# Two attention layers in one pass: normalizations placed by a sum of ScalarE's work, group means in phases of their own, tasks not cut at a unit's end, products of zeros at the start, an earlier last reciprocal

## The chip, the core and the metric

The kernel runs on one core of a Trainium2 chip, as one launch. The metric is the device time in microseconds (us) of that launch. In the profile PE is TensorE's matrix multiplication, PEld its weight loads, ACT is ScalarE, DVE is VectorE, POOL is GpSimd, and SP is the engine whose queue issues most of the DMA transfers. The clock given with the profile is the share of full speed that TensorE was granted.

## What is computed

The input is x of shape (4, 256, 64, 64) in float32. Two layers are applied, each behind a group normalization over 32 groups of 8 channels, each with 8 heads of 32 channels, each added to its input:

```
x = x + layer0(group_norm(x))
    q = Wq.h                      (256 -> 256, at 4096 positions)
    k, v = 2x2 convolutions of h, stride 2   (1024 positions)
    k = k + rel_h + rel_w
    out = softmax(q.k / sqrt(32)) . v        (4096 x 1024 per head)
x = x + layer1(group_norm(x))
    q, k, v = 1x1 projections of h + bias
    attention inside each of 4 areas of 1024 positions
    out = out + depthwise 7x7 convolution of v + bias
    out = Wproj.out + bias
```

## The kernel before, in words

**Units and phases.** Layer 0 of a batch is called ("A", b), layer 1 ("B", b). The order is A0 to A3, then B0 to B3. Each of these eight blocks has 16 units, one for 512 queries of four heads, so there are 128 units. A unit has 8 steps, one for each 128 keys. The main loop runs over phases, 683 of them, and a phase does one step and a half: a full step (512 queries) and a half step (256 queries). So a unit ends in about every fifth phase.

In one phase TensorE makes the scores (tile `s`, L400, three pairs of PSUM banks). ScalarE turns them into exponentials (`p`, L442 twice and L453 once). TensorE then multiplies the previous phase's exponentials with v (tile `av`, L467), and VectorE adds exponentials up (`acc`, L477). Where the previous phase's parts belong to two units, the phase has a cut: the first unit's av ends, ScalarE copies it out (`av_sb`, L1099), and the second unit's av begins. Later the sums are reduced by a product with ones (`den`, L486), copied (`den_sb`), turned into reciprocals by way of DRAM on POOL's queue, and multiplied in.

**Side work.** The projections q, k, v, the output projection (`ops`), the values for the convolution (`vals_ps`) and the convolution itself (`conv_ps`) are tasks. A task has two or four parts. A part is four products of 512 columns, or the same amount in another shape. Between the scores and av of a phase the loop does a number of parts of the task in front; `side_parts(n)` does up to n parts of one task. How many is decided from `pressure()` (what the due times demand), `supply()` (what will be there to do) and a credit. A phase with den does no other part. Side tasks write one PSUM bank, av another; where a cut comes and no task is begun, the two banks change roles (`banks.reverse`), so that the new unit's av need not wait for the copy.

**What feeds the tasks.** Each task reads a normalized chunk. A normalization is one ScalarE instruction (`taps`, `hq`, `hv`, `h`, L364), listed in `norms_left` with a first phase; `norm_next()` does the first one that is due, once at the end of each phase. A task is ready a phase after its last normalization. The group statistics come from `bn_stats` (L543, L656) and are joined in `plan_norm`: aggregation on VectorE, a product with `gmat` for the group means (`gm`, L334), a copy, three VectorE steps, a second product (`gv`, L342), then the power, the product and the sign on POOL. The two products are put in the list `quick`, and the loop takes one at a phase's end where no task is begun.

**Queues.** The order on every engine is the order in which the loop writes instructions. SP's queue is in order too, and carries the chunk loads (`xs`, `xa`, `hq`, `xc`, `hv`, `cv`, `xm`, six buffers of one pool), the layer 1 loads, the stores, and the convolution's rows and bands (`load_share`, issued inside `convolve`). A convolution is ready when both its shares were loaded at least 4 phases ago (`chained`).

**The end.** `project_last` calls `divide` for the last unit, which takes the reciprocal of the last den (L496, one VectorE instruction over 512 columns), multiplies, and the last projection follows.

These few lines stand at the loop's end, and the change replaces them:

```
        if quick and not begun():
            quick.popleft()()
        ...
        norm_next()
        for _ in range(max(parts, 2) - 2 if f < 12 else 0):
            norm_next()
```

Of the kernel before, what the change touches and what calls it, by code (L numbers as in the profile page):

```python
# [15 lines left out]
P = 128  # L16
# [44 lines left out]
def direct_path(  # L61
# [89 lines left out]
    gmat = gmat.rearrange("p g e -> p (g e)")  # L151
    neghalf = const.tile([P, CT], FP, name="neghalf")
    G.memset(neghalf, -0.5)
    ones = const.tile([P, HD], FP, name="ones")
    G.memset(ones, 1.0)
    eps = const.tile([P, 1], FP, name="eps")
# [27 lines left out]
    def at(g, j, f):  # L184
        g, j = g + int(j // NKT), int(j % NKT)
        plan.setdefault((g, j), []).append(f)
# [68 lines left out]
    def advance():  # L255
        side[0][0] -= 1
        side[0][2] = True
        next(side[0][1], None)
        if side[0][0] == 0:
            side.popleft()  # L260

    def need(made, key):
        while key not in made:
# [6 lines left out]
        return bool(side) and side[0][2]  # L270

    norms_left, norm_done = [], {}

    def later(token, f, start=0, first=False):

# [37 lines left out]
    def stats_of(key):  # L313
        if key not in stats:
            stats[key] = pool.tile([P, CT, NCH, 6], FP, tag="st", name=f"st_{key[0]}{key[1]}", bufs=2)
        return stats[key]

    def plan_norm(key, g, j):

        name = f"{key[0]}{key[1]}"  # L320
        made = {}

        def aggregate():
            for tag, cols in (("mv", 2), ("gmean", 1), ("dev", 1), ("gvar", 1)):
                shape = [P, CT, cols] if cols > 1 else [P, CT]
                made[tag] = pool.tile(shape, FP, tag=tag, name=f"{tag}_{name}", bufs=2)
            mv = made["mv"]
            for t in range(CT):
                V.bn_aggr(out=mv[:, t, :], in_=stats[key][:, t].rearrange("p c s -> p (c s)"))

        def means():
            mv, mean, dev = made["mv"], made["gmean"], made["dev"]
            ps = ps_side(f"gm_{name}")[:, :CT]
            T.matmul(ps, lhsT=gmat, rhs=mv[:, :, 0], start=True, stop=True)  # L334
            S.copy(mean, ps)
            V.tensor_sub(dev, mv[:, :, 0], mean)
            V.tensor_mul(dev, dev, dev)
            V.tensor_add(dev, dev, mv[:, :, 1])

        def variances():  # L340
            ps = ps_side(f"gv_{name}")[:, :CT]
            T.matmul(ps, lhsT=gmat, rhs=made["dev"], start=True, stop=True)  # L342
            S.activation(made["gvar"], ps, AF.Identity, bias=eps)
            norm = pool.tile([P, 2, CT], FP, tag="norm", name=f"norm_{name}", bufs=8)
            shift, rstd = norm[:, 0, :], norm[:, 1, :]
            G.tensor_tensor(rstd, made["gvar"], neghalf, ALU.pow)
            G.tensor_tensor(shift, made["gmean"], rstd, ALU.mult)
            G.tensor_scalar(shift, shift, -1.0, None, ALU.mult)
            norms[key] = shift, rstd

        at(g, j, aggregate)
        at(g, j + 1, lambda: soon(means))
        at(g, j + 3, lambda: soon(variances))

    def normalize(key, dst, src, t, by_vector=False):
        while key not in norms:
# [134 lines left out]
    def divide(g, unit):  # L491

        if g == len(units) - 1:

            rb = pool.tile([P, CH], FP, tag="p", name="rb", bufs=PB)
            V.reciprocal(rb, dens[g])  # L496
            V.tensor_mul(unit[4]()[:, unit[0], :], avs.pop(g), rb)  # L497
            spare.extend((dens.pop(g), rb))
            return
        den_sb = pool.tile([P, CH], FP, tag="cout", name="den_sb", bufs=2)  # L500
        few = pool.tile([P, 2, CH // HD], FP, tag="few", name="few", bufs=2)
        rows = dram.tile([4, CH], FP, tag="rows", name=f"rows_{g}", bufs=4)
        S.copy(den_sb, dens.pop(g))
        G.dma_start(rows, den_sb[0:P:HD, :])
        G.dma_start(few[:, 0, :], rows.rearrange("h (q n) -> (h q) n", n=CH // HD))  # L505
        made = {}

        def reciprocals():
            rb = made["rb"] = pool.tile([P, CH], FP, tag="rb", name="rb", bufs=1)
            recs = dram.tile([4, CH], FP, tag="recs", name=f"recs_{g}", bufs=4)  # L510
            V.reciprocal(few[:, 1, :], few[:, 0, :])
            V.tensor_reduce(sums[:, :, g], few, AX.X, ALU.add)  # L512
            G.dma_start(recs.rearrange("h (q n) -> (h q) n", n=CH // HD), few[:, 1, :])  # L513
            for h in range(4):
                G.dma_start(rb[HD * h : HD * h + HD, :], recs[h : h + 1, :].to_broadcast([HD, CH]))  # L515

        def multiply():
            V.tensor_mul(unit[4]()[:, unit[0], :], avs.pop(g), made["rb"])  # L518

        at(*((g + 2, 1) if g < len(units) - 2 else (g + 1, 6)), reciprocals)  # L520
        at(g + 2, 6 if g < len(units) - 2 else 0, multiply)
# [7 lines left out]
    def plan_a(b, u, prep):  # L529

        key = ("A", b)

        early = prep - (5 if b == 1 else 7 if b else 0)
        areas = {}

        seen = {}
# [66 lines left out]

        for c in range(NCH):
            at(early + c // 2, 4 * (c % 2), lambda c=c: look(c))
            at(early + c // 2, 4 * (c % 2) + (6 if b else 3), lambda c=c: add_stats(c))
        plan_norm(key, early + 4, 3 if b > 1 else 4 if b else 1)
        for a in range(NAREA):
            g = prep + (1 + 3.6 * a if b == 1 else 0.05 + 3.7 * a if b else 6 + 2.2 * a)
            at(0, int(NKT * (g - 2.4)), lambda a=a: load(a))  # L610
# [432 lines left out]
    def plan_conv(b, n, start):  # L1043
        when = int(start * NKT)
        room = 3 if b else 2
        for _ in range(room if n == 0 else 0):
            at(0, when - 8, lambda: len(loaded) < room and load_share(True))
        def chained():
            return all(k in loaded and loaded[k][2] + 4 <= phase[0] for k in ((b, 2 * n), (b, 2 * n + 1)))

        task_at(when, 2, convolve, b, n, due=start + 2.5, ready=chained, lag=3)

    units = []
    for i, (layer, b) in enumerate(BLOCKS):
# [38 lines left out]
        if weights_left[g] <= 2 * (NKT - 1):  # L1093
            opened.add(g)

    def evict(g):
        if weights_left[g] == 0 and g in av_of:
            avs[g] = pool.tile([P, CH], FP, tag="av", name="av_sb", bufs=2)
            S.copy(avs[g], av_of.pop(g))  # L1099

# [31 lines left out]
    while f < PHASES or before or plan or side or quick or norms_left or to_add or to_divide:  # L1132
# [13 lines left out]
            accumulate(s, u)  # L1146
        if cut:
            evict(before[0][0] // NKT)
        exps[2]()
        _, rate = pressure()  # L1150
        parts = 0
        if due and not begun():
            g = to_divide.popleft()
            divisors(g, *([last - 1] if g == final else []))
            if g < final:
                divide(g, units[g])
        else:
            wanted = credit + max(min(supply(), 2.0), min(rate, 2.0))
            if rate > 2:
                parts = side_parts(4)  # L1160
            elif rate > 1.5 or due or f >= PHASES or wanted >= (0.8 if cut else 1.5):
                parts = side_parts(2)
            elif wanted >= 0.5 and not cut or begun():
                parts = side_parts(1)
            credit = max(-0.5, min(wanted - parts, 0.5))
# [4 lines left out]
        add_ready()  # L1170
        if f >= PHASES:
            side_parts(2)
        if quick and not begun():
            quick.popleft()()
        while step < -(-3 * (f + 1) // 2):
            do(*divmod(step, NKT))
            step += 1
        norm_next()
        for _ in range(max(parts, 2) - 2 if f < 12 else 0):
            norm_next()  # L1180
        if before:
            evict(before[-1][0] // NKT)
        before = mine
# [599 lines left out]
```

## Time and profile before

| what | us |
|---|---|
| median of 4 runs | 3131.12 (3128.14 to 3135.19) |
| the profiled execution | 3126.19 |
| its span, from the first to the last instruction | 3124.5 |
| mean granted TensorE clock | 0.995 |
| TensorE waits: gm for mv, once, at the start | 17.1 |
| conv_ps for rows, 5 times | 10.6 |
| s for p (L442), 15 times | 10.5 |
| av for av_sb, 18 times | 8.7 |
| mean of one exponential of 1024 columns (L442) | 1.025 |
| mean of one add of 1024 columns (L477) | 1.219 |
| mean of one normalization: taps, hq, hv, h | 0.652, 0.846, 0.840, 1.263 |
| mean of a copy: av_sb, den_sb | 0.592, 0.607 |

A line of the timeline has the start, the length, the engine, the source line, the operation, what is written and read, the shape, and how many records in a row; in brackets the engine's idle time before it and what ended that. Each product stands as two records. Starts of consecutive lines show the pace better than their lengths, since one instruction's end overlaps the next one's start.

### The profile page before, as it was taken

How to read it: one execution, taken by the hardware profiler on the slowest of the kernel's cores; microseconds unless marked ns; L12 is line 12 of the kernel's file. 1: busy time of each engine (PE TensorE's matmuls, PEld its weight loads, DVE VectorE, ACT ScalarE, POOL GpSimd, SP SyncE). 2: the span in 40 equal slices, each digit the busy share in tenths (PEclk: the TensorE clock that was granted, in tenths of full speed). 3: DMA queues.
4: the chain of work that ended last, by engine and by line, in shares of the span. 5: the costliest groups of instructions: out<-in, count | busy, mean ns of one | idle time of the engine just before them, and what ended most of it. 6: DMA issues, size and time to landing. Idle time of an engine off the chain costs nothing. (4 is left out here: it accounts for less than half of the span.)

```text
span 3124.5 us, 109786 instructions
## 1 busy us (share of the span) xinstructions
PE 3043.3 (97%) x47138; PEld 1257.4 (40%) x47138; DVE 2518.0 (81%) x2719; ACT 2456.1 (79%) x2988; POOL 482.7 (15%) x923
## 2 busy tenths in 40 slices
PE   7999999999999999999999999998999999999997
PEld 3444344443344444344344444443434343333332
DVE  3788988778887787778688887776888888888888
ACT  3888888887888888878788787785777877778885
POOL 0111121111211111111112111111111111111111
PEclk9999999999999999999999999999999999999999
DMA  5244433555344466777767567667755465542232
GB/s 187 58 100 102 109 93 83 113 137 145 87 121 133 129 175 168 178 199 190 198 167 183 160 161 193 163 165 177 172 134 129 117 158 131 141 109 73 56 69 61
DMA packets 648322, 423.70 MB, mean 136 GB/s; under 512 B 411772, under 2 KB 556636, under 8 KB 647832
## 3 DMA queue, kind: packets, MB, share of 16 engines
q1 hardware_dynamic: 619384, 380.11, 47.9%
q0 software_dynamic: 28448, 36.48, 4.9%
q8 instruction: 378, 6.19, 0.9%
q14 instruction: 112, 0.92, 0.1%
HBM read 318.32 MB, written 98.09 MB: 133 GB/s over the span
## 5 line engine op out<-in xcount | busy, mean ns | idle before, releaser
L477 DVE TENSOR_TENSOR acc<-acc,p 128x1024 f32<-128x1024 f32 x1790 | 2114.1, 1219 | 457.6 <-PE av L467 220.4
L442 ACT ACTIVATE p<-s 128x1024 f32<-128x1024 f32 x1194 | 1160.4, 1025 | 445.6 <-PE s L400 429.6
L453 ACT ACTIVATE p<-s 128x1024 f32<-128x1024 f32 x598 | 618.8, 1035 | 1.3 <-DVE acc L477 0.8
L400 PE MATMUL s<-q,k_B 32*64 32x512 f32 (+1 forms) x10912 | 547.8, 498 | 8.1 <-ACT p L442 7.0
L400 PE MATMUL s<-q,k_A 32*64 32x256 f32 (+1 forms) x10928 | 546.6, 497 | 5.3 <-ACT p L442 3.5
L467 PE MATMUL av<-p,v_A 128*32 128x256 f32 (+1 forms) x4784 | 453.1, 488 | 0.0
L467 PE MATMUL av<-p,v_B 128*32 128x512 f32 (+1 forms) x4776 | 449.6, 487 | 0.0
L400 PEld LDWEIGHTS s<-q,k_B 32*64 32x64 f32 x10912 | 261.3, 130 | 348.4 <-issue 146.1
L400 PEld LDWEIGHTS s<-q,k_A 32*64 32x64 f32 x10928 | 261.5, 130 | 341.1 <-issue 140.5
L515 POOL DMA_DIRECT2D rb<-recs x508 | 252.1, 502 | 497.6 <-DMA recs<-few 411.9
L513 POOL DMA_DIRECT2D recs<-few x127 | 70.0, 551 | 1361.7 <-DVE sums L512 1202.2
L467 PEld LDWEIGHTS av<-p,v_B 128*32 128x32 f32 x4776 | 149.7, 110 | 261.4 <-issue 235.7
L467 PEld LDWEIGHTS av<-p,v_A 128*32 128x32 f32 x4784 | 152.0, 110 | 234.2 <-issue 194.7
L442 ACT ACTIVATE acc<-s 128x1024 f32<-128x1024 f32 x172 | 167.1, 1023 | 86.8 <-PE s L400 86.8
L505 POOL DMA_DIRECT2D few<-rows x127 | 71.4, 562 | 472.6 <-DMA rows<-den_sb 464.8
L486 PE MATMUL den<-acc,ones 128*32 128x512 f32 x1024 | 140.1, 606 | 2.8 <-DVE acc L477 2.7
L165 PE MATMUL ops<-cv,wp_sb 128*32 128x512 f32 x1024 | 126.5, 605 | 7.1 <-DVE cv L793 4.4
L165 PE MATMUL q1ps<-h,wqkv_sb 128*32 128x512 f32 x1024 | 126.6, 605 | 4.6 <-DVE xm L808 4.6
L165 PE MATMUL k0ps<-taps,wkv 128*32 128x256 f32 x2048 | 125.0, 385 | 2.5 <-ACT taps L364 2.5
L165 PE MATMUL k1ps<-h,wqkv_sb 128*32 128x512 f32 x1024 | 123.9, 597 | 1.8 <-ACT k_B L710 1.6
L165 PE MATMUL q0ps<-hq,wq_sb 128*32 128x512 f32 x1024 | 125.3, 598 | 0.0
L165 PE MATMUL vals_ps<-hv,wqkv_sb 128*32 128x512 f32 x1024 | 123.4, 597 | 0.0
(99 smaller groups left out, 2122.6 us busy)
## 6 DMA issues: line engine op xcount, KB each, us to landing
rows<-vals SPq DMA_DIRECT2D x384, 195.9 KB
rb<-recs POOLq DMA_DIRECT2D x508, 64.0 KB, 3.6
share<-vals SPq DMA_DIRECT2D x128, 195.9 KB
vala<-vout SPq DMA_DIRECT2D x128, 144.0 KB
vals<-vout SPq DMA_DIRECT2D x128, 144.0 KB
vc<-vala SPq DMA_DIRECT2D x64, 288.0 KB
band<-mats SPq DMA_DIRECT2D x96, 176.0 KB
hq<-in_x SPq DMA_DIRECT2D x32, 512.0 KB
```

The costliest lines, as they stand in the source:

```text
L165: T.matmul(out[cols, :], lhsT=lhsT[:, cols], rhs=rhs, start=start, stop=stop)
L400: T.matmul(out[n : n + WIDE], lhsT=unit[2]()[rows, unit[0], j * P + n : j * P + n + WIDE], rhs=unit[1]()[rows, cols], start=True, stop=True,)
L442: S.activation(p, (a, b)[n], AF.Exp, scale=SCALE)
L453: S.activation(p, c.rearrange("p b (l n) -> p b l n", l=2), AF.Exp, scale=SCALE)
L467: T.matmul(out, lhsT=v[:, j, unit[0] * P + HD * h : unit[0] * P + HD * h + HD], rhs=rhs, start=(j == 0 and not u), stop=(j == NKT - 1), sk ...
L477: V.tensor_add(to, to, p)
L486: T.matmul(dens[g][HD * h : HD * h + HD, :], lhsT=ones, rhs=p(h), start=(n == 0), stop=(n == len(sets) - 1),)
L505: G.dma_start(few[:, 0, :], rows.rearrange("h (q n) -> (h q) n", n=CH // HD))
L513: G.dma_start(recs.rearrange("h (q n) -> (h q) n", n=CH // HD), few[:, 1, :])
L515: G.dma_start(rb[HD * h : HD * h + HD, :], recs[h : h + 1, :].to_broadcast([HD, CH]))
```

## The change

It makes these edits, all in the planning code; the products, exponentials and transfers are the same ones, apart from the products of zeros.

- **Account.** `copies` counts ScalarE's extra instructions of a phase (task ends, den, av copies, normalizations), and `behind` carries over what did not fit. `busy(products)` is the sum in us: 0.65 for each, 0.2 for the phase, less 0.857 for each side part. At a phase's end normalizations are done while `busy` with one more (0.75) stays within 0.3 plus 0.1 for each one listed; in the first 20 phases, in the last ones, or when 4 parts or fewer are ready to be done, one is done in any case.
- **Group means.** A `quick` entry takes the place of side work in a phase without den, without a begun task and without a cut, instead of being added to a phase.
- **No half task ahead of a unit's end.** If the begun task has an odd number of parts left, one part is done. In the phase before a cut, two parts are done or none.
- **Products of zeros.** For A0 alone, 44 products of a 128 x 128 tile of zeros are placed ahead of the first group product, and 14 more around the two group products. A0's shift is made by one VectorE instruction in place of two on POOL.
- **Last reciprocal.** It is written where the last den is made.
- **Plan.** For batches 2 and 3 the statistics' loads start one unit earlier, and for these the `bn_stats` stand two steps later behind their loads; the group products are placed accordingly. A convolution waits 6 phases behind its loads instead of 4, and is expected 5 phases later instead of 3.

```
+    idle = const.tile([P, P], FP, name="idle")
+    V.memset(idle, 0.0)
...
         if side[0][0] == 0:
             side.popleft()
+            copies[0] += 1
...
+    def busy(products, more=0.0):
+        return max(0.0, behind[0] + 0.2 + copies[0] * 0.65 + more - 0.857 * products)
...
+    def keep_busy(n):
+        ps = ps_pair("idle")[:, 0, :P]
+        for _ in range(n):
+            T.matmul(ps, lhsT=idle, rhs=idle, start=True, stop=True)
...
+            if key == ("A", 0):
+                V.scalar_tensor_tensor(shift, made["gmean"], -1.0, rstd, ALU.mult, ALU.mult)
+            else:
                 G.tensor_tensor(shift, made["gmean"], rstd, ALU.mult)
                 G.tensor_scalar(shift, shift, -1.0, None, ALU.mult)
...
+        if key == ("A", 0):
+            at(g - 1, 0, lambda: keep_busy(44))
         at(g, j, aggregate)
-        at(g, j + 1, lambda: soon(means))
-        at(g, j + 3, lambda: soon(variances))
+        at(g, j + 1, lambda: soon(lambda: quietly(means, 4)))
+        at(g, j + 3, lambda: soon(lambda: quietly(variances, 10)))
...
-            rb = pool.tile([P, CH], FP, tag="p", name="rb", bufs=PB)
-            V.reciprocal(rb, dens[g])
-            V.tensor_mul(unit[4]()[:, unit[0], :], avs.pop(g), rb)
-            spare.extend((dens.pop(g), rb))
+            V.tensor_mul(unit[4]()[:, unit[0], :], avs.pop(g), spare[1])
...
-        early = prep - (5 if b == 1 else 7 if b else 0)
+        early = prep - (5 if b == 1 else 8 if b else 0)
...
-            at(early + c // 2, 4 * (c % 2) + (6 if b else 3), lambda c=c: add_stats(c))
-        plan_norm(key, early + 4, 3 if b > 1 else 4 if b else 1)
+            at(early + c // 2, 4 * (c % 2) + (6 if b == 1 else 8 if b else 3), lambda c=c: add_stats(c))
+        plan_norm(key, early + (5 if b > 1 else 4), 1 if b != 1 else 4)
...
-            return all(k in loaded and loaded[k][2] + 4 <= phase[0] for k in ((b, 2 * n), (b, 2 * n + 1)))
-        task_at(when, 2, convolve, b, n, due=start + 2.5, ready=chained, lag=3)
+            return all(k in loaded and loaded[k][2] + 6 <= phase[0] for k in ((b, 2 * n), (b, 2 * n + 1)))
+        task_at(when, 2, convolve, b, n, due=start + 2.5, ready=chained, lag=5)
...
             if g < final:
                 divide(g, units[g])
+            else:
+                rb = pool.tile([P, CH], FP, tag="p", name="rb", bufs=PB)
+                V.reciprocal(rb, dens[g])
+                spare.extend((dens.pop(g), rb))
+        elif quick and not begun() and not cut and f < PHASES:
+            quick.popleft()()
         else:
             wanted = credit + max(min(supply(), 2.0), min(rate, 2.0))
...
+            elif begun() and side[0][0] % 2:
+                parts = side_parts(1)
+            elif boundary(mine):
+                parts = side_parts(2) if wanted >= 0.9 else 0
             elif wanted >= 0.5 and not cut or begun():
                 parts = side_parts(1)
...
-        if quick and not begun():
+        if quick and f >= PHASES:
             quick.popleft()()
...
-        norm_next()
-        for _ in range(max(parts, 2) - 2 if f < 12 else 0):
-            norm_next()
+        if before:
+            evict(before[-1][0] // NKT, True)
+        work = max(parts, done_den)
+        force = f >= PHASES or f < 20 or pressure()[0] <= 4
+        while norms_left and (force or busy(work, 0.75) <= 0.3 + 0.1 * len(norms_left)) and norm_next():
+            copies[0] += 1
+            force = f >= PHASES
+        behind[0], copies[0] = min(busy(work), 0.4), 0
```

## Prediction

> **What bounds the kernel now.** I read the page's busy shares, then TensorE's waits, then TensorE's timeline phase by phase.
>
> ```profile
> PE 3043.3 (97%) x47138; PEld 1257.4 (40%) x47138; DVE 2518.0 (81%) x2719; ACT 2456.1 (79%) x2988; POOL 482.7 (15%) x923
> ```
>
> TensorE is the bound, so only what shortens its own sequence counts. The loop has 683 phases. I took each from its first score product (s) to the next phase's. A phase with one side part (den included) takes 3.794 us (the median, 261 phases in program order), with two parts 4.653 (399), with none 3.173 (17); within a kind most agree to 0.01 us. So a second part adds 0.859, a first on top of the bare 3.794 - 0.859 = 2.935 likewise, and a phase without side work wastes 3.173 - 2.935 = 0.238: there the exponentials set the pace. Phases run from 72.4 to 3093.5. Summed at these prices (conv and k0/v0 parts, 0.01 to 0.06 dearer, at their own) they come to 2945.8; the trace has 3021.2. The other 75.3 us lie in some 70 places. The first kind is a half task ahead of a unit's end:
>
> ```profile
> 2606.16 1.58 PE L400 MATMUL s<-q,k_B 32*64 32x256 f32 x32
> 2607.67 1.06 PE L165 MATMUL k1ps<-h,wqkv_sb 128*32 128x512 f32 x8
> 2608.55 1.47 PE L467 MATMUL av<-p,v_B 128*32 128x512 f32 x16
> 2609.95 1.58 PE L400 MATMUL s<-q,k_B 32*64 32x256 f32 x32
> 2611.46 0.64 PE L467 MATMUL av<-p,v_B 128*32 128x256 f32 x8
> 2611.92 1.04 PE L165 MATMUL k1ps<-h,wqkv_sb 128*32 128x512 f32 x8
> 2613.60 1.07 PE L467 MATMUL av<-acc,v_B 128*32 128x512 f32 x8 [0.65 <-ACT av_sb L1099]
> 2614.60 1.58 PE L400 MATMUL s<-q,k_B 32*64 32x256 f32 x32
> ```
>
> The first phase lasts 2609.95 - 2606.16 = 3.79. In the second the task's other half holds the side bank, so the new unit's av must wait until the old one is copied out: 4.65 for one part, 0.85 too much. There are 16 such cuts, 0.42 to 0.85 each, together 10.5 us. Second, the phase behind one without side work:
>
> ```profile
> 1683.75 1.58 PE L400 MATMUL s<-q,k_B 32*64 32x256 f32 x32
> 1685.26 1.06 PE L467 MATMUL av<-p,v_B 128*32 128x512 f32 x8
> 1686.14 0.61 PE L467 MATMUL av<-acc,v_B 128*32 128x256 f32 x8
> 1686.92 1.12 PE L400 MATMUL s<-q,k_B 32*64 32x256 f32 x16 [0.17 <-ACT p L442]
> 1688.33 1.09 PE L400 MATMUL s<-q,k_B 32*64 32x512 f32 x16 [0.29 <-ACT acc L453]
> ...
> 1691.63 1.58 PE L400 MATMUL s<-q,k_B 32*64 32x256 f32 x32
> ```
>
> The empty phase takes 3.17, the next, with den alone, 4.71 instead of 3.79: ScalarE is behind, and its scores wait twice. This follows every one of the empty phases: eight with den next cost 0.85 on average, seven with other work next 0.43, one followed by another empty one 0.19; together 10.0. Third, the convolution waits for its rows:
>
> ```profile
> 1514.29 1.06 PE L1023 MATMUL conv_ps<-share 88*32 88x128 f32 x32
> 1520.27 0.66 PE L1023 MATMUL conv_ps<-rows,band 88*32 88x128 f32 x8 [4.92 <-DMA rows<-vals]
> 1523.03 1.52 PE L1023 MATMUL conv_ps<-rows,band 88*32 88x128 f32 x24 [2.10 <-DMA rows<-vals]
> 1526.18 1.81 PE L400 MATMUL s<-q,k_A 32*64 32x256 f32 x32
> ```
>
> This phase (from 1512.33) takes 13.85 for 4.72, with the one at 1346.8 and its successor 16.1 in all; part of it is the clock, 0.67 of full speed in 1520 to 1530. The rest: 12 group products, 7.0; a stall chain at 2127 to 2155 (VectorE sits 10.3 for vc<-vala, then ScalarE for VectorE), 13.8; den waiting for VectorE's adds at 698.9 and 1571.3, 6.6; a normalization waiting for hv near 1478, 2.7; small ones 8.6.
>
> **The change, part by part.** Places are counted in the two programs' instruction orders; work is equal but for products of zeros.
>
> Half tasks (the odd-remainder and boundary branches): cuts with one part fall from 16 to 1. 10.5 - 0.4: -10.1.
>
> The price stands beside it: phases without side work rise from 17 to 41, since parts are held back at boundaries and means and variances get phases of their own. 24 x 0.238 = 5.7. Behind them: 13 have den next (13 x 0.85 = 11.1), 17 other work (17 x 0.43 = 7.3), 10 an empty one (10 x 0.19 = 1.9), one ends the loop: 20.3 less 10.0 = +10.3. Together +16.0. The lower bound is +5.7, if the account keeps ScalarE from being behind; the upper 24 x (0.238 + 0.85) = +26. I take the rows' own prices, because ScalarE's new order still has av_sb, den_sb and a normalization side by side at four of the 13, as at three of the rows of 0.91 now.
>
> Group products: of the 12, 11 get empty phases and one stays beside two parts. Now they cost 0.31 to 0.33 beside two parts, 0.55 to 1.20 beside den or one part, where they wait for a bank that is still to be copied (496.84: 0.70 behind den_sb). In an empty phase no bank is pending. 12 x 0.15 = 2 left, between 0 and 12 x 0.31 = 3.7: -5 (-7 to -3).
>
> Convolution (lag 5, chained +6): loads in program order lie at least 4 phases before use now (20 of 128 at 4), then at least 5, all but one 6 and more. Two phases are at least 2 x 3.79 = 7.6; the longest overrun is 4.92 + 2.10 = 7.0. That covers it, with the same SP order around: -14 (-16 if nothing remains, -5 if the transfers are later still). Its tasks stretch (phases 305 to 400 for the second batch, 296 to 376 now), and none comes within 20 phases of its first reader except the last batch, where five phases remain before cv<-conv is issued.
>
> Statistics for b of 2 and 3: xs loads one unit earlier, bn_stats two steps later. VectorE's wait of 2.39 for xs at 694.7 precedes the 5.1 at 698.9: -4 (0 to -6.6). The cost is a chunk slot held two steps longer; behind it on SP's queue stand hq, hv, cv and xm, which need slots of that pool.
>
> Normalizations by the account: one per phase now, later only when ScalarE's sum allows it or few tasks are pending. Behind a late one wait the tasks that read it. Two show it: q0 of batch 3 is forced inside a score group at phase 277 (new; the other forced place shrinks from three tasks to two), and at five places two tasks share a phase. The nearest row is 0.81 (k1ps waiting for k_B, near 2181): +2 (0 to +4). The gain for the hv wait: -1 (0 to -2.7).
>
> The chain at 2127: the change touches neither vc<-vala nor its place; convolutions stand at phases 449, 455, 462 as against 448, 454, 461. It depends on how late SP is: -4 (0 to -13.8).
>
> Head. The two first k0 blocks take 8.71 for 2 x 3.63: 1.45 of cold clock; gm and gv 0.56 + 0.59 for 0.38 each: 0.39; two POOL steps (20.31 to 20.83) against one on VectorE, idle until the result, of 0.16: 0.36. Best -2.2. A zero product costs between 0.23 (a 256-column k0 product, 3.63/32, times four for four strips, halved) and 0.37 (two weight loads of 0.186), double while cold. From about 1 us, 44 of them end between 13 and 19, and gm is due at 17.08: up to +2 if late. I take -1. [...]
>
> Tail: the reciprocal goes ahead of the 0.75 step that waits for TensorE:
>
> ```profile
> 3102.77 1.16 DVE L793 SCALAR_TENSOR_TENSOR cv<-cv,bpe_sb,att_B 128x512 f32<-128x512 f32 x1
> 3104.89 0.75 DVE L808 SCALAR_TENSOR_TENSOR xm<-ops,bproj_sb,xm 128x512 f32<-128x512 f32 x1 [0.97 <-PE ops L165]
> 3105.56 3.35 DVE L496 RECIPROCAL rb<-den 128x512 f32<-128x512 f32 x1
> ```
>
> Only the idle 0.97 goes, since both steps still precede att: -1 (to -2.7 if the clock then stays up).
>
> Sum: -10.1 + 16.0 - 5 - 14 - 4 + 2 - 1 - 4 - 1 - 1 = -22.1. Against the profiled execution's 3126.19 (span 3124.5 and 1.7 around it): 3104.1. The median of the runs, 3131.12, is 4.9 above that execution: 3109.
>
> **Rivals.**
> 1. The transfers all come right: the 2127 chain and the adds vanish too (-13.8 - 6.6 - 2.7 for the -9 above): 14 less, 3095. For it: fewer loads in flight at once. Against: SP's order near 2127 is the same.
> 2. A wash: empty phases at +26, conv at -5, group products at -3. 22.1 - 10 - 9 - 2 leaves -1, 3130. For it: 41 empty phases are a large count. Against: those prices are the ends.
> 3. Slower: normalizations held back keep chunk slots, SP's in-order queue stands, and transposes come late as at 2127. The place would be batches 2 and 3 of the first layer, phases 250 to 400, where SP also waits now (391.8 us for out<-xm alone). One such chain is 13.8; two eat the gain, and three give 3131.1 - 22.1 + 41.4 = 3150. It decides from the second. Against: SP's waits mostly hide, and the conv spacing relieves the queue there.
> 4. Zero products do nothing or harm: 3 us at most, inside the range.
>
> **How the numbers follow.** About 0.2% (6 us) is what this kernel's measurement can tell from no change. Forecast 0.52, its own range 3095 to 3122; rival 1, 0.20; rival 2, 0.14; rival 3, 0.14. The range reaches to rival 1's further side, and over rival 2's time: 3088 to 3133. Faster: 0.52 + 0.20 and a third of rival 2: 0.77; same 0.09; slower 0.14.
>
> **What would show it.** TensorE's list of waits: av for av_sb near 2 us (8.7 now); conv for rows under 2 (10.6); scores for p up, to some 20 (10.5), each behind an empty phase. k0's first 128 records near 7.3. The half-clock windows at 1352 and 1520 gone. Wrong if scores wait less for p than now (empty phases are cheap: 3095), or if conv, or VectorE for vc, waits 10 us or more somewhere new (rival 3).

## The result, and the profile after

The changed kernel takes 3131.93 us (median of 49 runs, 3126.14 to 3140.72) against 3131.01 for the kernel before (74 runs beside them): ratio 1.0005, 95% interval 1.0000 to 1.0011. Forecast were 22 us less; there is no gain that can be measured. The profiled execution has a span of 3132.6 us, 8.1 above the one of before, whose own time lay 4.9 below its median.

The busy shares of the page of after:

```profile
PE 3068.4 (98%) x47254; PEld 1270.8 (41%) x47254; DVE 2517.8 (80%) x2721; ACT 2458.0 (78%) x2988; POOL 483.9 (15%) x921
```

ScalarE and VectorE work as long as before, within 2 us; nothing was added that costs by itself. PE is busier by 25 us, 18.5 of them the products of zeros at the start. So the answer is in the waits. TensorE's list of waits, after (what waited, for what; us in all, times, the longest):

```profile
PE s L423 <- ACT p L465: 23.8, 22, 6.2
PE den L509 <- DVE acc L500: 6.0, 4, 3.3
PE k1ps L167 <- ACT k_B L730: 3.0, 3, 1.4
...
PE gm_B L347 <- DVE mv_B L342: 2.0, 2, 1.0
...
PE av L490 <- ACT av_sb L1122: 0.6, 1, 0.6
```

Two signs came as foretold: av waits 0.6 us for its copy instead of 8.7, and the convolution's wait for rows (10.6) has left the list. The scores wait 23.8 us for p; about 20 were foretold, but 16.3 of them are three single waits, of 5.2, 6.2 and 4.8 us, and none of them comes behind an empty phase. ScalarE's own list of waits for data, after, names what they are:

```profile
ACT hv L387 <- DMA hv<-xmid: 11.5, 4, 6.5
ACT hq L387 <- DMA hq<-in_x: 7.1, 2, 6.0
ACT hv L387 <- POOL norm_B L364: 6.0, 1, 6.0
```

Before, the only such wait above 1.6 us was for hv (7.6 in all, the longest 3.9). The longest of after, in ScalarE's and then TensorE's timeline:

```profile
1380.84 0.61 ACT L523 COPY den_sb<-den 128x512 f32<-128x512 f32 x1
1387.95 0.81 ACT L387 ACTIVATE hv<-hv,norm_B 128x512 f32<-128x512 f32 x1 [6.50 <-DMA hv<-xmid]
1388.67 1.92 ACT L465 ACTIVATE p<-s 128x1024 f32<-128x1024 f32 x2
```

```profile
1380.58 1.58 PE L423 MATMUL s<-q,k_A 32*64 32x256 f32 x32
1382.09 1.06 PE L167 MATMUL vals_ps<-hv,wqkv_sb 128*32 128x512 f32 x8
1382.97 1.47 PE L490 MATMUL av<-p,v_A 128*32 128x256 f32 x16
1390.64 2.04 PE L423 MATMUL s<-q,k_A 32*64 32x256 f32 x20 [6.19 <-ACT p L465]
```

ScalarE's order is fixed, so a normalization whose chunk has not landed holds up the exponentials behind it (6.50 us here), and the scores wait for their banks (6.19). The prediction's wait for conv_ps was TensorE's own; this one is the same stall one engine further on.

The whole loop, taken phase by phase with the prediction's prices (3.173, 3.794, 4.653 for none, one and two parts); what a phase takes above its price goes to the row of what it waited for. In us, one profiled execution each:

```
                                        before   after
head (to the first phase)                 72.4    72.0
phases at their prices                  2942.9  2948.4
cuts with a half task                      9.7     0.8
convolution waits for rows                15.3     0
ScalarE waits for late data                3.9    22.5
VectorE waits for a transfer              21.4    16.7
the phase behind an empty one              8.2    16.4
phases with group products                 7.8     8.9
all else above the price                  12.0    17.2
tail                                      30.9    29.7
span                                    3124.5  3132.6
```

The row of ScalarE counts the phases in which it waits for a transfer or for `norm_B`, the scale and shift that the group products lead to; the longer phase right behind such a stall is not in it. So 5.3 of the 22.5 us are the wait for `norm_B` at 507, where the kernel before has 1.5 of its 3.9. The phases are sorted anew here, so a row can differ from the prediction's by up to 2 us.

These are single executions, and rows may shift by a few us: the first group mean alone begins between 15.96 and 18.15 us in the executions profiled here, as the first loads land. The kernel before had medians from 3116 to 3133 us on the chips used, so the experiments are compared by their ratio to the kernel before on the same chip; the rows of the table serve to see where the time lies. The changed kernel was not timed beside the experiments, so what one edit is said to be worth in it is a difference of two ratios, 1.0005 and the experiment's, and rests on the ratio being the same on every chip. Two experiments on one chip can be set against each other without that.

### The profile page after: what moved, and what is told of

It reads as the page before. It is cut to its first block, busy times and chain, and to the rows that moved or that the text cites. A ratio compares the mean times of both kernels' runs of the same rounds, so it can differ in the third digit from the quotient of the medians.

```text
span 3132.6 us, 110020 instructions
## 1 busy us (share of the span) xinstructions
PE 3068.4 (98%) x47254; PEld 1270.8 (41%) x47254; DVE 2517.8 (80%) x2721; ACT 2458.0 (78%) x2988; POOL 483.9 (15%) x921
## 3 DMA queue, kind: packets, MB, share of 16 engines
q8 instruction: 378, 6.19, 0.8%
## 5 line engine op out<-in xcount | busy, mean ns | idle before, releaser
L423 PE MATMUL s<-q,k_A 32*64 32x256 f32 (+1 forms) x10928 | 556.0, 501 | 23.8 <-ACT p L465 21.5
```

The lines of the kernel that those rows point to most:

```text
L423: T.matmul(out[n : n + WIDE], lhsT=unit[2]()[rows, unit[0], j * P + n : j * P + n + WIDE], rhs=unit[1]()[rows, cols], start=True, stop=True,)
```

## The experiments

Four undo one part of the change (the diffs are against the changed kernel). First the account:

```
-        if before:
-            evict(before[-1][0] // NKT, True)
...
-        behind[0], copies[0] = min(busy(work), 0.4), 0
+        norm_next()
+        for _ in range(max(parts, 2) - 2 if f < 12 else 0):
+            norm_next()
```

> The changed kernel, with the old rule for normalizations (one at each phase's end) in place of the account. Late-data theory (the account writes normalizations into ScalarE's in-order stream before their chunk or their mean is there, and the exponentials behind them stand still: 22.5 us of phase excess against 3.9 before): 18 to 25 us less than the changed kernel, 3107 to 3114. Spacing theory (loads are late because the wider spacing of the convolutions holds the band buffers and SP stands on them): no change, 3125 to 3138, the waits stay. Empty-phase theory (41 phases without side work are what ate the gain): no change either.

Measured: 1.0041 (1.0027 to 1.0055). The account is worth 0.36%, some 11 us, where the prediction gave it a loss of 1; none of the three expectations had the kernel slower without it. ScalarE's waits for late data stay at 19.8 us without it, so it isn't their cause.

The convolution's spacing as before:

```
-loaded[k][2] + 6 <= phase[0]
+loaded[k][2] + 4 <= phase[0]
...
-ready=chained, lag=5)
+ready=chained, lag=3)
```

> The changed kernel, with the convolutions' old spacing (4 phases behind their loads, expected after 3). Spacing theory: ScalarE's waits for hv and hq fall to about 4 us, waits for rows come back with about 15; together 3125 to 3130, and SP's wait for conv_ps falls from 427 to about 330 us. Late-data theory: ScalarE's waits stay, rows come back: 3140 to 3148.

Measured: 0.9983 (0.9966 to 1.0000). Waits for rows are back (11.2 us of phase time), ScalarE's late data fall from 22.5 to 5.6, of which 5.0 are the wait for `norm_B`, and SP's wait for conv_ps falls from 427.0 to 331.6. These are the signs of the spacing theory. With the old spacing the kernel is no slower, rather faster.

The group products added to a phase as before:

```
-        elif quick and not begun() and not cut and f < PHASES:
-            quick.popleft()()
...
-        if quick and f >= PHASES:
+        if quick and not begun():
             quick.popleft()()
```

> The changed kernel, with the group products added to a phase with side work again instead of having phases of their own. Empty-phase theory: about 11 phases without a part fewer; floor -2.6, excess behind them -3 to -5, the products themselves as before (7.8): 3120 to 3126. Late-data theory alone: no change beyond that, ScalarE's waits near 22 us stay.

Measured: 0.9956 (0.9940 to 0.9973), the largest gain of one edit. In its profile the normalization that waits 6.0 us for norm_B at 507 is gone, and of the ones for loads at 1380 and 1504 none above 1.9 us is left. A new one stands at 1247, where gm_B waits 4.2 us for its bank and two phases cost 9.5 us more than their price. Two later pairs, each on one chip, undo the same edit where late loads were mended first, and it gains less: 0.22% with the early loads mended, 0.25% with the longer distance as well, both with overlapping intervals. So part of the 0.49% seems to come from the loads that land in time in this run; that wasn't tested by itself.

Without the two rules on half tasks:

```
-            elif begun() and side[0][0] % 2:
-                parts = side_parts(1)
-            elif boundary(mine):
-                parts = side_parts(2) if wanted >= 0.9 else 0
```

> The changed kernel, without the two rules that keep half tasks from a unit's end. Half-cut rows of before: 10 us come back; phases without a part fall by some 10 and give back 2.4 of floor and 4 to 6 behind them. So 3131 to 3138 if a held-back part costs less than a half cut, under 3131 if it costs more.

Measured: 1.0019 (1.0010 to 1.0029). The cuts cost 11.5 us again, but empty phases fall from 41 to 34 and what lies behind them from 16.4 to 11.9: the rules are worth 0.14%, a net of 4 us out of a term of 10, with an interval that just touches the changed kernel's. In the expectation's terms a held-back part costs less than a half cut.

**Where the late data come from.** SP's queue in the changed kernel (start, length of the issue, line, transfer), ahead of the wait at 1387.95:

```profile
1343.02 2.12 SPq L1027 DMA_DIRECT2D rows<-vals  x4
1345.24 0.42 SPq L1024 DMA_DIRECT2D band<-mats  x1
1345.70 3.60 SPq L1027 DMA_DIRECT2D rows<-vals  x4
1350.21 0.39 SPq L1055 DMA_DIRECT2D conv<-cout  x1
1364.91 0.30 SPq L1024 DMA_DIRECT2D band<-mats  x1
1365.26 1.62 SPq L1027 DMA_DIRECT2D rows<-vals  x4
...
1379.42 2.22 SPq L950 DMA_DIRECT2D hv<-xmid  x1
```

From 1350.6 to 1364.9 SP stands, 13.8 us of it for conv_ps: a third share of batch 0 is to be loaded into a pool with two buffers, and waits for the next convolution. The rule of the early loads asks for up to three shares ahead of batch 1's first convolution. The wider spacing moves batch 0's last convolutions past that point, so the third share is still one of batch 0, which has no third buffer. The hv load stands behind it, is issued 26.6 us after its phase began, and ScalarE gets there first. The edit that takes this away alone:

```
-            at(0, when - 8, lambda: len(loaded) < room and load_share(True))
+            at(0, when - 8, lambda: len(loaded) < (room if shares and shares[0][0] else 2) and load_share(True))
```

> The changed kernel with one edit: the loads ahead of a batch's first convolution may not put a third share of batch 0 into its two buffers. Theory (the wider spacing of the convolutions makes these early loads meet batch 0's last shares, so SP stands at a band until the next-but-one convolution, and the hv loads behind it come late to ScalarE): SP's wait for conv_ps, 427 us in the changed kernel, falls below 350; excess of phases in which ScalarE waits for loaded data falls from 22.5 us to about 8; no wait for rows comes back; ratio to the kernel before about 0.996, where the changed kernel stands at 1.0005. Rival (the loads are late because shares are held longer in general, whatever is loaded ahead): these waits stay above 15 us and the ratio stays above 0.9985.

Measured: 0.9966 (0.9953 to 0.9979). SP's wait for conv_ps falls from 427.0 to 347.6 us, ScalarE's for hv from 11.5 to 1.8, and no wait for rows returns. Its SP queue at the same place:

```profile
1340.21 0.45 SPq L1024 DMA_DIRECT2D band<-mats  x1
1342.09 3.33 SPq L1027 DMA_DIRECT2D rows<-vals  x4
1346.36 1.46 SPq L975 DMA_DIRECT2D vala<-vout  x2
...
1361.49 2.40 SPq L950 DMA_DIRECT2D hv<-xmid  x1
1363.99 0.33 SPq L1024 DMA_DIRECT2D band<-mats  x1
```

The standing is gone, and hv goes out 15.4 us behind its phase instead of 26.6. The row of late data fell only to 18.1, though, not to the expected 8, and stays above the rival's 15: the waits for hq (7.1) and for `norm_B` at 507 stay, and the phase at 1950 costs 5.3 us above its price, where it cost 2.6.

The two edits together (early loads as above, group products as before):

> The changed kernel with the group products added to a phase as in the kernel before, and with the early loads kept to two shares of batch 0. Theory (two separate costs): the ratio of the first edit alone, 0.9956, falls by another 0.3 to 0.5%, to about 0.992; ScalarE's waits for loaded data about 8 us, rows none. Rival (the two edits act on the same late loads, so that the second adds nothing): 0.995 to 0.997.

Measured: 0.9944 (0.9925 to 0.9963), between the two expectations, and not to be told from the group products alone or from the early loads alone.

**The parts by themselves, on the kernel before.** The spacing alone (6 phases, lag 5):

> The kernel before with the wider spacing of the convolutions alone (6 phases behind the loads, 5 phases expected). Theory (the stall moves from TensorE's wait for rows to SP's queue and so to ScalarE): the 15 us of waits for rows vanish, ScalarE's waits for loaded data rise from 3.9 us to 12 or more, ratio 0.998 to 1.001. Rival (as predicted: the wider spacing by itself gains, and ScalarE's late data come of the account or the statistics' earlier loads): ratio near 0.9955, ScalarE's waits stay under 6 us.

Measured: 0.9994 (0.9982 to 1.0007). The waits for rows are gone altogether, and ScalarE's late data rise from 3.9 to 17.5. Its two places in ScalarE's timeline:

```profile
1349.26 0.63 ACT L503 COPY den_sb<-den 128x512 f32<-128x512 f32 x1
1355.96 0.81 ACT L364 ACTIVATE hq<-hq,norm_A 128x512 f32<-128x512 f32 x1 [6.07 <-DMA hq<-in_x]
...
1941.30 0.71 ACT L710 ACTIVATE k_B<-k1ps,bqkv_sb 128x512 f32<-128x512 f32 x1
1952.46 1.24 ACT L364 ACTIVATE h<-h,norm_B 128x1024 f32<-128x1024 f32 x1 [10.45 <-DMA h<-xmid]
```

So the stall moves from TensorE to ScalarE by the spacing alone, without account, statistics or group products. Both loads stand in SP's queue behind the ten transfers of a convolution's two shares: hq goes out 20.8 us after its phase began, and may be awaited 4 phases (at most 18.6 us) behind it. The next run keeps the spacing, adds the edit of the early loads, and lets the normalizations `taps` and `hq` of layer 0 and `hv` of layer 1 come 5 phases behind their loads, for example:

```
-fetched["q", c] + 4
+fetched["q", c] + 5
```

> The kernel before with the wider spacing of the convolutions, the early loads kept to two shares of batch 0, and the normalizations of layer 0 not before 5 phases behind their loads. Theory (the wider spacing gains 14 us as soon as the loads queued behind a convolution's are not awaited too early): the wait of 6.1 us for hq at 1349 us goes, the one of 10.5 us for h at 1942 us may stay (its start is planned apart), ratio 0.9955 to 0.998 where the spacing alone stands at 0.9994. Rival (the wait only moves on to the next reader of late loads): ScalarE's waits for loaded data stay above 12 us, ratio 0.9985 to 1.0005.

Measured: 0.9974 (0.9964 to 0.9984). The wait for hq is gone, the one for h stays (9.1), as the theory had it. The row of late data ends at 13.1, above the rival's 12, mostly because of that wait for h. That the spacing is what gains here is not shown: the stall at 698.9, which stands in the run with the spacing alone (5.0 us), is gone too, and no run has the two edits of the loads without the spacing.

The half-task rules alone:

> The kernel before with the two rules on half tasks alone. Theory (cuts give 10 us, phases without side work take most of it back): half cuts go from 9.7 us to under 1, phases without side work rise from 17 to 25 or more, ratio 0.998 to 1.0. Rival (empty phases cost little, since ScalarE catches up in them): ratio 0.9965 to 0.997.

Measured: 0.9995 (0.9979 to 1.0011). No half cut costs anything any more, 27 phases are empty (17 before), behind them 14.7 us (8.2), and 2.4 more at the prices. That is 9.7 less against 8.9 more: the two halves of the trade cancel.

The account alone:

> The kernel before with the account of ScalarE's work alone. Theory (undoing the account in the changed kernel cost 0.36%, so alone it gains about as much, by ScalarE being less often behind at a cut or a den): ratio 0.996 to 0.9975, scores wait less for p than the 10.5 us of before. Rival (the account only repairs what the empty phases of the other edits cause; the prediction gave it +1 us): 0.9995 to 1.0005.

Measured: 0.9974 (0.9959 to 0.9988). Scores wait 5.8 us for p instead of 10.5, and the stall of 5.1 at 698.9 is gone, with the statistics' loads where they were: VectorE waits 0.29 us for xs there instead of 2.39. With that the phase costs 4.6 us less, where the two profiled spans differ by 5.3, so most of the gain seen is not ScalarE being less often behind at a cut or a den. Why the xs load lands in time was not traced.

Group products in phases of their own alone:

> The kernel before with the group products in phases of their own alone. Theory (in such a phase the product stands ahead of av, before VectorE has made mv and dev, so TensorE waits about 1 us at each, and the copy of the means comes behind an exponential; a dozen such phases and the normalizations behind them): gm waits for mv in the list of waits, group phases 1 us above the price of an empty one, ratio 1.003 to 1.005. Rival (the 0.5% that undoing it gained needs the other edits, the late normalization at 507 us above all): 0.999 to 1.001. By the prediction's -5 us: 0.9985.

Measured: 1.0015 (1.0002 to 1.0029), between the expectations, and on the other side from the prediction. The price in such a phase can be read from the changed kernel, here at 490:

```profile
490.30 1.58 PE L423 MATMUL s<-q,k_A 32*64 32x256 f32 x32
492.88 0.35 PE L347 MATMUL gm_B<-mv_B,gmat 128*128 128x2 f32 x2 [1.00 <-DVE mv_B L342]
493.16 1.50 PE L490 MATMUL av<-p,v_A 128*32 128x512 f32 x16
494.59 1.58 PE L423 MATMUL s<-q,k_A 32*64 32x256 f32 x32
```

The product stands between the scores and av, and is there 1.00 us before VectorE has made mv. The phase takes 4.29 for the 3.17 of an empty one. To see whether this place is the cost, the product was kept in a phase of its own but written behind av:

```
         elif quick and not begun() and not cut and f < PHASES:
-            quick.popleft()()
+            own = True
...
-        if quick and f >= PHASES:
+        if quick and own:
             quick.popleft()()
```

> The changed kernel with its group products in phases of their own as before the edit, but written behind av at the phase's end. Theory (in its own phase the product stands ahead of av, before VectorE has made mv or dev, and its copy comes behind an exponential, which costs 1 us in each of a dozen phases): group phases at the price of an empty one plus 0.2, gm no longer waits for mv, ratio 0.997 to 0.9985 where the changed kernel stands at 1.0005. Rival (the cost lies in the order behind it, the normalization at 507 us that waits for POOL's power): that wait of 6 us stays, ratio 0.9995 to 1.001.

Measured: 0.9992 (0.9981 to 1.0004), 0.13% under the changed kernel, with overlapping intervals. The phase at 487 now takes 3.31, gm_B waits for mv nowhere, and the row of group phases falls from 8.9 to 4.2 us. The wait for norm_B stays (6.4). So both expectations hold in part, and what was left was traced in POOL's timelines, first of the changed kernel, then of the one with group products as before:

```profile
506.05 0.55 POOL L533 DMA_DIRECT2D recs<-few  x1 [10.60 <-DVE sums L532]
510.59 1.98 POOL L535 DMA_DIRECT2D rb<-recs  x4 [3.99 <-DMA recs<-few]
512.59 0.74 POOL L359 TENSOR_TENSOR norm_B<-gvar_B,neghalf 128x2 f32<-128x2 f32 x1
```

```profile
501.93 1.17 POOL L359 TENSOR_TENSOR norm_B<-gvar_B,neghalf 128x2 f32<-128x2 f32 x1 [13.91 <-ACT gvar_B L356]
503.19 0.19 POOL L363 TENSOR_TENSOR norm_B<-gmean_B,norm_B 128x2 f32<-128x2 f32 x1
503.47 0.22 POOL L364 TENSOR_SCALAR norm_B<-norm_B 128x2 f32<-128x2 f32 x1
503.93 0.63 POOL L533 DMA_DIRECT2D recs<-few  x1 [0.24 <-issue]
```

In the changed kernel the second product found no phase of its own before the first normalization that needs it came due; `normalize` then writes it on the spot (at 507.24, instead of 501.16 with the group products as before), and the normalization stands directly behind it in ScalarE's order. The power falls behind the reciprocals' transfers on POOL's in-order queue: POOL waits for recs to land until 510.59, and ScalarE, ready at 507.9, has norm_B at 513.95. In the other order the power goes first. With the group products' own phases alone, ScalarE's wait at this place is 2.0 us of phase time (1.5 in the kernel before), and without the account in the changed kernel 2.2. In the changed kernel it is 5.3, and 2.5 in the phase behind: the two edits meet here. That the queue order by itself is worth them was not tried.

**The rest.** Without the products of zeros:

```
-        if key == ("A", 0):
-            at(g - 1, 0, lambda: keep_busy(44))
...
-            if key == ("A", 0):
-                keep_busy(n)
```

> The changed kernel without the products of zeros. Theory (they warm the clock for the first k0 blocks): the two first k0 blocks take 8.7 us again, where they take 7.3 or a little more with them; the stretch ahead of the first phase grows by 1 to 2 us; the ratio rises by 0.0003 to 0.0007 above the changed kernel's 1.0005. Rival (they delay the group means as much as they give): the stretch ahead stays at 72 us.

Measured: 1.0015 (1.0001 to 1.0029), 0.1% above the changed kernel, with overlapping intervals. The first k0 blocks in TensorE's timeline, after, then without the zeros:

```profile
18.82 3.33 PE L329 MATMUL idle<-idle 128*128 128x128 f32 x14
22.09 7.79 PE L167 MATMUL k0ps<-taps,wkv 128*32 128x256 f32 x128
```

```profile
20.19 9.84 PE L167 MATMUL k0ps<-taps,wkv 128*32 128x256 f32 x128 [2.07 <-ACT taps L383]
```

They take 2.05 less with the zeros in these two executions, 0.9 against the execution of before, and 7.79 is not the 7.3 foretold. The granted clock shows why. In the window from 17 to 23 us (busy time of PE, PEld, DVE, ACT, POOL; granted clock; DMA share and rate) of the changed kernel, then of the one with group products as before:

```profile
17.00:23.00 6.00, 5.90 (x34) 5.22 (x38) 2.03 (x8) 2.94 (x8) 0.72 (x1) 0.50 1.11 337
```

```profile
17.00:23.00 6.00, 5.41 (x74) 4.20 (x78) 2.02 (x8) 3.76 (x9) 0.72 (x1) 1.00 1.09 342
```

In the changed kernel's execution the records of the zero products start 0.21 us apart at first and 0.11 apart from 6.54 us on; the clock records begin there, at 6.45, with full clock. The zeros end at 14.63, ahead of gm at 16.48, and the clock stands at 0.50 from 16.69 to 23.52. In the other execution it is 1.00 throughout the window, and the same blocks take 7.11. The stretch to the first phase hardly shows the gain (72.2 without, 72.0 with the zeros), because with them the k0 blocks begin 1.90 later: 0.34 by the first group mean (16.48 against 16.14), the rest behind the last zero products, which take 3.33 us at half clock (1.81 in the execution where the clock stays up). That is the rival's sign.

Statistics of batches 2 and 3 where they were:

```
-        early = prep - (5 if b == 1 else 8 if b else 0)
+        early = prep - (5 if b == 1 else 7 if b else 0)
...
-            at(early + c // 2, 4 * (c % 2) + (6 if b == 1 else 8 if b else 3), lambda c=c: add_stats(c))
-        plan_norm(key, early + (5 if b > 1 else 4), 1 if b != 1 else 4)
+            at(early + c // 2, 4 * (c % 2) + (6 if b else 3), lambda c=c: add_stats(c))
+        plan_norm(key, early + 4, 3 if b > 1 else 4 if b else 1)
```

> The changed kernel with the statistics' loads and bn_stats of batches 2 and 3 where they were. Theory (the earlier loads remove VectorE's waits near 695 us, as predicted, 4 us): those waits of 2.4 and 5.1 us come back, ratio 1.0015 to 1.0025. Rival (the chunk slots held two steps longer make later loads of that pool late): SP's waits and ScalarE's waits for loaded data fall below the changed kernel's 22.5 us, ratio 0.997 to 1.0.

Measured: 1.0029 (1.0015 to 1.0043). The edit is worth some 0.24%, but not where it was foretold: the waits near 695 us do not come back. What grows is ScalarE's late data (30.8 for 22.5) and one group phase at 400 (3.5 us above its price, gv waiting 1.9 for dev). Why these loads, of batches 2 and 3, shift the later ones is open.

**Towards a better kernel.** The changed kernel with the edit of the early loads and 5 phases between load and normalization:

> The changed kernel with the early loads kept to two shares of batch 0, and normalizations of layer 0 not before 5 phases behind their loads instead of 4. Theory (with the wider spacing ten transfers of a convolution stand together on SP's queue, 20 us behind the program, and ScalarE reaches hq at 1484 us before the load has landed): ScalarE's wait for hq, 7.1 us with 4 phases, falls under 2; ratio 0.994 to 0.9955 where the first edit alone stands at 0.9966. Rival (what is left comes of the account or the group products, the loads being late by more than a phase): the wait stays above 5 us, ratio 0.996 to 0.998.

Measured: 0.9957 (0.9941 to 0.9973). The wait for hq is gone; the time is lower than with the first edit alone, but the intervals overlap. With the group products as before as well:

> The same with the group products added to a phase as in the kernel before: the changed kernel with its three costs taken out. Theory (they are separate): ratio 0.991 to 0.9935, ScalarE's waits for loaded data under 6 us. Rival (the stalls stand for one another, so that taking the next away gives less): 0.994 to 0.996.

Measured: 0.9932 (0.9915 to 0.9950), faster than the kernel before (3112.66 us against 3132.59 on that chip) and, by the ratios, than the changed one. The ratio fell within the theory's bounds, its second sign did not: ScalarE's late data stand at 18.7 in the profiled execution, where vout waits three times for its earlier values to be stored (7.8 in all) and hv five times for xmid (6.6).

## Why the prediction was wrong

- **Half tasks, -10.1, and empty phases, +16.0: right.** The cuts went from 9.7 to 0.8 us. 24 more empty phases cost 5.5 at the prices and 8.2 behind them, 13.7 for 16.0.
- **Convolution, -14: this step failed.** Its sentence was that two phases of 7.6 us cover the longest overrun of 7.0 "with the same SP order around". The rows' waits did vanish (15.3 to 0). But the order around was not the same: the loads move on SP's queue against the normalized chunks, the early loads meet batch 0's last shares in two buffers, and ScalarE's row of late data rises by 18.6 us, 3.8 of them for `norm_B` and the rest for transfers. The spacing alone moves the stall at no gain (0.9994), and without it the changed kernel's row is 5.6. With two edits of the loads beside it 0.26% are gained; how much of that is the spacing's stays open. The prediction counted the loads' distance to their own reader, and not what waits behind them.
- **Group products, -5: wrong in sign.** "In an empty phase no bank is pending" was true and not the question. The product waits for its input, mv or dev, up to 1 us, and where no free phase comes in time, the second product is written only when its normalization is due, so that ScalarE waits for POOL's whole chain (6.0 us at 507). Undoing it gains 0.49% in the changed kernel, about 15 us, and 0.22 to 0.25% where the late loads were mended; alone it costs 0.15%.
- **Account, +2 and -1: wrong.** It gains 0.26% alone and 0.36% in the whole, 8 to 11 us. The sum looked at the late readers alone. In the profile with the account alone the gain is mostly the stall at 698.9; what makes the 0.36% in the changed kernel stays open.
- **Statistics, -4: a gain of the right sign (0.24%), by another way.** The stall at 698.9, which carried the step, goes with the account alone, and is gone as well with the early statistics where the account is undone: either takes it away, so undoing one doesn't bring it back.
- **The chain at 2127, -4:** "the change touches neither vc<-vala nor its place", yet VectorE's wait of 10.3 there went to 2.3 with the spacing alone. What is left of the chain after is 6.6 of 13.8 us, and 16.0 stand there in the changed kernel with the old spacing. So here the spacing did relieve the queue, by more than the term allowed.
- **Head, -1, and tail, -1:** -0.4 and -1.2. In the head the clock was at 0.50 from 16.69 to 23.52 us, and the first k0 blocks began in that stretch, at 22.09.

The two failed terms, conv and group products, made 19 of the 22 us forecast, and the waits that they brought on ScalarE and POOL used up what the others gained. As an estimate from the runs that undo one part: account, statistics, rules and zeros gain 0.36 + 0.24 + 0.14 + 0.10 = 0.84%, spacing and group products cost 0.22 + 0.49 = 0.71%. The parts meet, so this is no exact account. Rival 3 had the engine and the stretch (SP's in-order queue, the first layer's batches 2 and 3) but named the normalizations held back as the cause; undoing the account shows that they are not. Rival 2's time, 3130, was right by other prices than its own, which is luck. Among the signs, "conv, or VectorE for vc, waits 10 us or more somewhere new" looked for the new wait on the wrong engines. It was in ScalarE's list.

## What to carry to other kernels

When a load is moved away from its reader on an in-order queue, list the transfers that now stand behind it, and for each the instruction that will await it and how far that is planned behind; the time won at one reader can be lost at the next if that distance is shorter than the queue's lag (here 20 us of lag against 4 phases). A limit on loads ahead has to count the buffers of the pool that the next load will really use. And a small product put into a gap waits for its inputs there (1.00 us at 492.88): ask when they are made, before asking which bank is free.

## What the runs showed of the hardware

In the changed kernel TensorE's granted clock stood at 0.50 for 6.83 us at each of the three longest stalls: from 515.04 (a stall of 5.22 us, over at 516.63), from 1388.85 (6.19, over at 1390.64) and from 1511.73 (4.85, over at 1514.01). The scores behind each take 2.90 us where 1.58 is usual, so each of these stalls cost more than its length. In windows of the changed kernel (length; busy time of PE, PEld, DVE, ACT, POOL; granted clock; DMA share and rate):

```profile
1350.00:1360.00 10.00, 10.00 (x148) 3.37 (x136) 7.39 (x10) 9.81 (x14) 2.24 (x5) 1.00 0.58 157
1385.00:1395.00 10.00, 4.36 (x40) 1.50 (x44) 4.53 (x7) 6.53 (x8) 3.00 (x6) 0.69 0.82 231
1508.00:1518.00 10.00, 5.15 (x72) 2.35 (x68) 5.49 (x5) 6.68 (x9) 1.67 (x4) 0.69 0.64 159
```

The half-clock at 1352 and 1520 of before (0.66 in 1350 to 1360, 0.67 in 1520 to 1530) is gone with the rows' waits, as foretold (1.00 in both windows after), and stands at ScalarE's waits instead. Behind the stall of 6.19 us the next phase is 2.4 longer, behind that of 4.85 it is 2.1. In the clock records of the executions profiled before and after, each halved stretch lasts 3.41 us or 6.83, unless the program ends first. The length of a stall didn't decide alone there. In the changed kernel the first of these two was followed by 6.83 us at half clock (the scores behind it take 2.90 where 1.58 is usual), the second by none:

```profile
1261.62 2.90 PE L423 MATMUL s<-q,k_A 32*64 32x256 f32 x32 [1.97 <-ACT p L465]
2168.85 1.67 PE L509 MATMUL den<-acc,ones 128*32 128x512 f32 x5 [3.35 <-DVE acc L500]
```

Within one execution these stretches start whole multiples of 3.41333 us apart, to 0.01 us. Counted in such steps, the stall of 1.97 lies within one, from 1259.15, while that of 3.35 falls on two, from 2163.68 and 2167.09, with 1.59 and 1.79 us of idle time. The two executions have 1740 steps at full clock between 100 us behind the start and 30 before the end. The 1731 in which TensorE idled 1.79 us or less were followed by a step at full clock, the 9 in which it idled 1.97 us or more by one at half clock.
